# A fixed timetable for the sorted mixtures, three places for gathered rows, and the far bounds of images 0 to 2 moved into the last attention

## The chip, the cores and the metric

The kernel runs on one core of a Trainium2 chip. A core has a matrix engine (PE; its weight loads are listed as PEld), a vector engine (DVE), a scalar engine (ACT), a general engine (POOL), and a queue engine (SP) that issues most of the memory transfers. Each engine takes its own instructions strictly in the order in which they were built; semaphores make one engine wait for another, or for a transfer. The metric is the time of one execution in microseconds (us), the median of several runs. TensorE's clock is granted by a throttle, and the profile reports the granted share (1.0, or 0.5 in stretches where PE has been idle a good deal).

## The reference

Four images of 56 x 56 pixels with 128 channels go through four layers, of which three matter here.

- Layer 2 has a softmax attention over the 3136 pixels of each image, and then a mixture of eight experts: a router picks two experts for each pixel, and the two experts' outputs are added with normalised weights:

```python
top_p, top_i = jax.lax.top_k(router_probs, K)          # K = 2 of 8
expert_out = jnp.einsum('bnd,edc->bnec', x, expert_w) + expert_b
gathered = jnp.take_along_axis(expert_out, top_i[..., None], axis=2)
return jnp.einsum('bnk,bnkc->bnc', top_p, gathered)
```

- Layer 3 starts with an attention whose scores are `exp(-dist2)` of projected queries and keys, followed by a softmax over those scores:

```python
dist2 = q2[:, :, None] + k2[:, None, :] - 2.0 * qk
scores = jnp.exp(-GAMMA * dist2)
attn = jax.nn.softmax(scores, axis=-1)
return jnp.einsum('bqk,bkd->bqd', attn, V)
```

When every query is far from every key all scores are the same number, and the result is the plain mean of the values. The kernel adds that mean, and proves it by bounding all distances (the "bounds"); only if the proof fails does it run the full computation.

- Layer 3 ends with an "expert choice" step: for each of 64 experts the eight pixels with the largest router probability are gathered, sent through the expert, and scattered back.

## The kernel before

**Tiles.** An image is 28 tiles of 112 pixels (`NT`), in seven groups of four (`NG`, 448 columns). The layer-2 attention, `Attention.run` (L2372 on), goes through the four images one after the other. For each group it makes the queries (L2315, `z_ps`), and then takes 25 blocks of 128 keys: a product for the scores (L2339, `s_ps`), an exponential on ACT (L2346), and a product that adds up the results (L2422, `o_ps`). One block is one step; an image has 172 steps. When a group is done, `finish` scales and adds it (L2359 to L2368).

**Work beside the attention.** Everything else of that time is cut into small pieces, which are handed out between the steps. `background(i)` makes the list for the i-th image's attention, and `Paced` hands out the pieces: each piece has a stated cost, the costs are added up along the list, and a piece is due when the attention has done the same share of its first six groups. What is left then is handed out at once. A piece marked as apart waits for the next step if one of the same list has just been handed out. The order in which pieces are handed out is not yet the order of the instructions: a scheduler in the framework places each instruction on its engine by its own estimate of times, and the buffers limit it. One limit matters here: all pieces, the queries of the next group and the `finish` of the last one take their PSUM tile from a single ring of four (`flow.one`, L975), in the order in which they were handed out.

The lists of the four attentions are: for images 0 and 1, an earlier layer's recurrence; for image 2 (the third attention) the sorted mixtures of images 0 and 1, and the far part and the expert choice of image 0; for image 3 (the fourth and last attention) the sorted mixture of image 2, and the far part and the choice of images 1 and 2. Image 3's own mixture and far part follow its attention group by group (`trail`). After the fourth attention come the rest of image 3, the experts, and the scatter.

**The sorted mixture of one image** (`SortedMixture.pieces`) has three parts.

- *front*: statistics, router products and the two best experts of each pixel; then `ranks` and `whose` (L1784 to L1797) compute where each pixel's row goes when rows are sorted by expert. 112 small products (`id_ps`, two instructions each for 56 ids) end in the list of rows, `o_id`.
- *there*: 28 pairs of 128-row tiles. For pair c, `fetch` gathers its rows with two indirect DMAs on POOL (L1805) into a place of the ring "got" and writes them to DRAM (SP, L1809); `load` reads them back block-transposed with four DMAs (SP, L1817) and loads the two experts' weights, whose number is read into a register first (SP, L1825 and L1828); `apply` transposes on DVE (L1834), makes the two products `y_ps` (PE, L1838), copies them (ACT, L1843), and stores them (SP, L1844). That is eight DMAs of SP a pair. In the list, `fetch` of pair c stands with `load` of pair c-5 and `apply` of pair c-8.
- *back*: for each of 28 tiles two indirect DMAs on POOL gather the two experts' rows of each pixel (`bring`, L1852, into a ring of three `o_back` places), and DVE adds them to x (`put`, L1860). It needs all 28 stores of *there*.

The rings lie in one scratch tile: two places for gathered rows ("got"), three for transposed blocks ("xs"), three for weights ("w"), two each for the rest.

**The far part of one image** (`FarAttention.image`): for each group, normalised rows are transposed (L210), projected (L2098, L2103) and given their norms (L2121, L2122); then the mean of the values is added (L2165), and 175 bounds follow (L2134, `d_ps`, 32 x 448), half of them reduced by DVE (L2140) and half by ACT (L2146). **The expert choice of one image** (`ExpertChoice.pieces`) stores x, makes logits (L2600), finds and marks the eight best pixels (L2624 to L2636), gathers them and pools them.

The lists of the two last attentions read:

```python
lists = [
    merged(pieces, front0),
    merged(there0 + back0, front1),
    merged(there1, far0 + merged(add0 + chosen(0), bounds0)),
]                                                        # third
lists = [
    merged(held["back"], front),
    merged(there + back, far1 + merged(add1 + chosen(1), bounds1)),
    far, merged(add + chosen(2), bounds),
]                                                        # fourth
```

Of the kernel before, what the change touches and what calls it, by code (L numbers as in the profile page):

```python
# [40 lines left out]
NQ = EC // ET  # L41
SLOTS = 2 * TOK // 128 + NE - 1

PERIOD = (
# [1598 lines left out]
class SortedMixture:  # L1643

    def __init__(self, env, ctx, flow, mixture, scratch):
# [12 lines left out]
        self.rings, self.turn, at = {}, {}, 0  # L1658
        for name, n in (("got", 2), ("xs", 3), ("xsT", 2), ("w", 3), ("y", 2)):
            self.rings[name] = [scratch[:, at + i * 256 : at + (i + 1) * 256] for i in range(n)]  # L1660
            self.turn[name] = 0
            at += 256 * n
# [25 lines left out]
    def pieces(self, b):  # L1688
# [124 lines left out]
        def load(c):  # L1813
            xs = held["xs", c] = self.ring("xs")
            squares = given.rearrange("(f k) (a i) -> a k f i", k=32, i=32)
            for a in range(4):
                last = nc.sync.dma_start(  # L1817
                    xs[32 * a : 32 * (a + 1), :].rearrange("p (f i) -> p f i", i=32),
                    squares[a][:, 8 * c : 8 * (c + 1), :],
                )  # L1820
            w = held["w", c] = self.ring("w").rearrange("p (j c) -> p j c", j=2)
            for j in range(2):
                at = 2 * c + j
                with env.tc.issue_after(last.ins):
                    e = nc.sync.value_load(  # L1825
                        held["expert"][:, at : at + 1], min_val=0, max_val=NE - 1
                    )
                    last = nc.sync.dma_start(  # L1828
                        w[:, j, :], self.experts[bass.ds(e, 1)].rearrange("e d c -> (e d) c")
                    )  # L1830
# [33 lines left out]

        def lagging(n, *steps):
            listed = []
            last = max(lag for lag, _, _, _ in steps)
            for i in range(n + last):
                for lag, cost, step, apart in steps:
                    if 0 <= i - lag < n:  # L1870
                        listed.append(costing(cost, lambda step=step, i=i - lag: step(i), apart))
            return listed

# [3 lines left out]
        ]  # L1877
        return (
            front,
            lagging(SLOTS // 2, (8, 0.9, apply, True), (5, 0.1, load, False), (0, 2.0, fetch, False)),  # L1880
            lagging(NT, (3, 0.4, put, False), (0, 2.0, bring, False)),
        )

# [25 lines left out]
class Paced:  # L1909
# [6 lines left out]
    def step(self, share):  # L1916

        begun = set()
        while self.at < len(self.pieces):
            piece = self.pieces[self.at]  # L1920
            if share < 1 and (
                self.due[self.at] > self.total * share
                or getattr(piece, "apart", False) and getattr(piece, "list", None) in begun
            ):
                return
            piece()
            begun.add(getattr(piece, "list", None))
            self.at += 1


# [42 lines left out]
class FarAttention:  # L1973
# [16 lines left out]
    def __init__(self, env, ctx, flow, work):  # L1990
# [4 lines left out]

        self.even = ctx.enter_context(ExitStack())
        self.held = [
            stack.enter_context(env.tc.tile_pool(name=name, bufs=1, side="right"))
            for stack, name in ((ctx, "d_odd"), (self.even, "d_even"))
        ]  # L2000
# [66 lines left out]
    def image(self, b, spans, places="d"):  # L2067
# [5 lines left out]
        held = {"q": {}}  # L2073
        pool = self.held[1 - b % 2]

        def turned(g):
            if g == 0:
                held["sums"] = sp.tile([128, NG], F32, tag="x_sums", name="x_sums")
                held["k"] = pool.tile(
                    [128, (NG - 1) * P + LW], BF16, tag="k_near", name="k_near",  # L2080
                    bufs=2 if b % 2 else 1,
                )
# [138 lines left out]
class Attention:  # L2221
# [150 lines left out]
    def run(self, mains, first, background, trail):  # L2372
# [27 lines left out]
        for at in range(-AHEAD, len(steps)):  # L2400
# [12 lines left out]
            if (g, k) == (0, 0):  # L2413
                pieces, following, after = background(i)
                behind = Paced(pieces)
                tails = trail(i)
# [753 lines left out]
def layers_of_safe_scores(env: Env, f, soft):  # L3170
    with ExitStack() as ctx:
# [22 lines left out]
        def background(i):  # L3194
# [11 lines left out]
            elif i == 2:  # L3206
                pieces, out = both([], 3)
                front0, there0, back0 = listed_all(held["sorted"].pieces(0))
                front1, there1, held["back"] = listed_all(held["sorted"].pieces(1))
                far0, add0, bounds0 = mixed(0)  # L3210
                lists = [
                    merged(pieces, front0),
                    merged(there0 + back0, front1),
                    merged(there1, far0 + merged(add0 + chosen(0), bounds0)),
                ]
            else:
                front, there, back = listed_all(held["sorted"].pieces(2))
                far1, add1, bounds1 = mixed(1)
                far, add, bounds = mixed(2)
                lists = [  # L3220
                    merged(held["back"], front),
                    merged(there + back, far1 + merged(add1 + chosen(1), bounds1)),
                    far, merged(add + chosen(2), bounds),
                ]
            return sum(lists, []), out, after

        def mixed(b):
# [6 lines left out]
            )  # L3234

        def listed_all(parts):
            return [listed("mixture", part) for part in parts]

# [40 lines left out]
        with tc.manual_schedule(  # L3279
# [10 lines left out]
            mixing.close()  # L3290
            far.even.close()
            more = ctx.enter_context(tc.tile_pool(name="e_more", bufs=UNITS))
# [118 lines left out]
```

## Time and profile before

| what | us |
|---|---|
| median of 15 runs (2663.25 to 2679.07) | 2669.99 |
| the profiled execution, its own time | 2670.27 |
| its span, first to last instruction | 2668.5 |
| third attention, from its first queries (1216.4) to the fourth's (1767.9) | 551.5 |
| fourth attention, from its first queries to its second group's (1835.1) | 67.2 |
| from there to its last group's queries (2335.7) | 500.6 |
| from there to its last copied result (2422.2) | 86.5 |
| the rest: image 3, the experts, the scatter | 246.3 |

The points in time are those of the PE timeline's `z_ps` rows (L2315), two queries a group, and of DVE's last copy at L2359. An engine's "busy" time counts only executing instructions; a row "A <- B" in a table of waits says that A's engine sat idle until B released it. In the numbers of L2339 and L2422 each product appears as two records, since a 32-bit product takes two passes; a fully busy PE at full clock gets through one such product in 0.75 us (two records each of L2339 and L2422 follow each other every 1.50 us at 1834 to 1839).

### The profile page before, as it was taken

Reading aid. Unit: us, or ns where it says so; the run is one execution under the profiler, and the core shown is the slowest. Engines: PE = TensorE matmul, PEld = TensorE weight load, DVE = VectorE, ACT = ScalarE, POOL = GpSimd, SP = SyncE. Lnnn points to the kernel's source line nnn. Section 1 sums busy time; section 2 is a strip of 40 time slices with the busy share of each in tenths; the row PEclk is TensorE's granted clock in tenths of the full one; section 3 lists DMA queues with packets and bytes.
Section 4 is the critical chain, followed back from the end, with each engine's and each line's share of the span. In section 5 each row is a group of like instructions: output and inputs, shape, how many; then the busy total and the mean of one; then the engine's idle time right before and its main releaser. Section 6 shows DMA issues by size and latency. Waiting matters only on the chain.

```text
span 2668.5 us, 42254 instructions
## 1 busy us (share of the span) xinstructions
PE 2356.4 (88%) x14531; PEld 1296.6 (49%) x14531; DVE 1750.0 (66%) x4986; ACT 1593.1 (60%) x3469; POOL 609.8 (23%) x921
## 2 busy tenths in 40 slices
PE   6999999999999999999855689988989799795586
PEld 4777777764555555555433333444444333232134
DVE  5666999948979597985612547655754475775544
ACT  5999888757666566655322257833355566682584
POOL 4323354200000000000232652343332250011301
PEclk9999999999999999999966788997988699797587
DMA  5000000000000000001144235411143310100575
GB/s 134 14 7 2 2 2 2 2 9 1 1 1 1 1 1 1 1 17 27 50 122 113 58 85 115 97 46 44 50 109 89 72 32 4 25 5 0 170 275 188
DMA packets 248484, 131.74 MB, mean 49 GB/s; under 512 B 119544, under 2 KB 238355, under 8 KB 244164
## 3 DMA queue, kind: packets, MB, share of 16 engines
q1 hardware_dynamic: 236996, 107.23, 15.5%
q0 software_dynamic: 11264, 21.72, 3.1%
q8 instruction: 117, 1.92, 0.3%
q14 instruction: 107, 0.88, 0.1%
HBM read 88.50 MB, written 40.26 MB: 48 GB/s over the span
## 4 chain that ended last, share of the span: by engine, by line
PE 53%; DVE 6%; DMA 6%; ACT 4%; issue 3%; SPq 3%; POOL 3%; POOLq 0%; DVEq 0%; ACTq 0%
PE s_ps L2339 18%; PE o_ps L2422 17%; PE d_ps L2134 3%; DMA o_back<-o_y,o_slot 3%; ACT d_ps L2146 2%; PE xT_ps L210 2%; PE g_ps L1209 2%; PE y_ps L1605 1%; PE y_ps L1838 1%; SPq L1817 1%; PE l_ps L2600 1%; POOL o_back L1852 1%; DMA lot<-in_L_ffn_lots 1%; PE z_ps L2315 1%; PE l_ps L1545 1%
## 5 line engine op out<-in xcount | busy, mean ns | idle before, releaser
L2339 PE MATMUL s_ps<-zT,xnT 128*128 128x448 f32 (+1 forms) x1400 | 668.9, 567 | 14.8 <-DVE zT L2318 14.7
L2346 ACT ACTIVATE e<-s_ps 128x448 f32<-128x448 f32 x688 | 366.6, 542 | 492.1 <-PE s_ps L2339 429.4
L2422 PE MATMUL o_ps<-e,keep 128*128 128x448 f32 (+1 forms) x1376 | 652.0, 558 | 0.0
L2339 PEld LDWEIGHTS s_ps<-zT,xnT 128*128 128x128 f32 (+1 forms) x1400 | 244.4, 193 | 225.9 <-issue 174.8
L2422 PEld LDWEIGHTS o_ps<-e,keep 128*128 128x128 f32 (+1 forms) x1376 | 241.7, 192 | 203.3 <-issue 202.8
L2140 DVE TENSOR_REDUCE found<-d_ps 128x1 f32<-128x448 f32 x306 | 184.5, 618 | 151.8 <-PE d_ps L2134 150.1
L2146 ACT ACTIVATE d_ps<-d_ps,half 128x448 f32<-128x448 f32 (+1 forms) x394 | 238.7, 608 | 74.4 <-PE d_ps L2134 72.6
L1805 POOL DMA_INDIRECT taken<-o_x,o_id x168 | 161.2, 960 | 330.0 <-DMA o_g<-taken 210.4
L2134 PE MATMUL d_ps<-q_near,k_near 32*128 32x448 bf16 (+1 forms) x700 | 165.1, 403 | 43.8 <-ACT d_ps L2146 25.7
L1852 POOL DMA_INDIRECT o_back<-o_y,o_slot x168 | 157.7, 939 | 173.1 <-DMA o_y<-taken 83.8
L210 PE MATMUL xT_ps<-ident,xn 112*128 112x112 f32 x672 | 122.4, 292 | 70.5 <-ACT xn L1966 59.0
L1946 POOL TENSOR_TENSOR g_rs<-var,exponent 112x4 f32<-112x4 f32 x17 | 17.5, 1031 | 647.3 <-DVE var L1945 632.8
L1838 PE MATMUL y_ps<-taken 128*128 128x128 f32 x336 | 82.5, 351 | 81.4 <-DMA taken<-o_w 56.0
L210 PEld LDWEIGHTS xT_ps<-ident,xn 112*128 112x128 f32 x672 | 83.2, 153 | 145.3 <-ACT xn L1966 91.2
L2134 PEld LDWEIGHTS <-k_near 32*128 32x128 bf16 (+1 forms) x700 | 36.4, 94 | 202.7 <-issue 188.7
L1966 ACT ACTIVATE xn<-x,g_off,g_rs 112x128 f32<-112x128 f32 x220 | 92.6, 484 | 65.9 <-DVE g_off L1948 32.8
L1838 PEld LDWEIGHTS y_ps<-taken 128*128 128x128 f32 x336 | 64.8, 233 | 128.1 <-issue 83.1
L1834 DVE STREAM_TRANSPOSE taken<-taken 128x256 f32<-128x256 f32 x84 | 36.5, 438 | 114.8 <-DMA taken<-o_g 109.0
L1843 ACT COPY taken<-y_ps 128x256 f32<-128x256 f32 x84 | 30.9, 368 | 128.5 <-PE y_ps L1838 69.6
L784 PE MATMUL f_ps<-w_fc,h 128*112 128x128 f32 x896 | 104.8, 274 | 1.9 <-ACT h L775 1.6
L679 DVE TENSOR_TENSOR e<-e,band 112x1792 f32<-112x1792 f32 (+3 forms) x56 | 99.9, 1786 | 8.9 <-ACT e L672 8.9
L784 PEld LDWEIGHTS f_ps<-w_fc,h 128*112 128x112 f32 x896 | 99.8, 177 | 5.2 <-ACT h L775 4.8
(481 smaller groups left out, 4501.2 us busy)
## 6 DMA issues: line engine op xcount, KB each, us to landing
lot<-in_L_ffn_lots SPq DMA_DIRECT2D x32, 1024.0 KB
o_g<-taken SPq DMA_DIRECT2D x84, 128.0 KB
taken<-o_g SPq DMA_DIRECT2D x336, 32.0 KB
taken<-o_w SPq DMA_DIRECT2D x168, 64.0 KB
o_y<-taken SPq DMA_DIRECT2D x84, 128.0 KB
out_x<-x SPq DMA_DIRECT2D x28, 224.0 KB
x<-in_x SPq DMA_DIRECT2D x3, 1568.0 KB
o_x<-xn SPq DMA_DIRECT2D x21, 224.0 KB
```

Source lines behind the costliest of these rows:

```text
L210: self.nc.tensor.transpose(ps[:, j * P : (j + 1) * P], xn[:, j, :], self.ident[:P, :P])
L679: nc.vector.tensor_tensor(es, es, bands[stripes[i][1] == 0][:n].rearrange("p h r c -> p h (r c)").unsqueeze(2) .to_broadcast([n, NH, m, 8 ...
L784: nc.tensor.matmul(f_ps[:, j, :], h[:, k, j * P : (j + 1) * P], w_fc2[:, k, :], start=(k == 0), stop=(k == 3),)
L1805: nc.gpsimd.indirect_dma_start(got[:, j, :], None, rows, bass.IndirectOffsetOnAxis(ap=held["id"][:, at : at + 1], axis=0),)
L1838: nc.tensor.matmul(y_ps[:, j, :], xsT[:, j * 128 : (j + 1) * 128], w[:, j, :], start=True, stop=True,)
L1852: nc.gpsimd.indirect_dma_start(back[:, k, :], None, out, bass.IndirectOffsetOnAxis(ap=held["slot"][:, at : at + 1], axis=0),)
L2134: nc.tensor.matmul(d, held["k"][part, 128 * c : 128 * c + n], held["q"][g][part, :], start=True, stop=True,)
L2140: nc.vector.tensor_reduce(self.found[:, self.most : self.most + 1], d, AX.X, ALU.max)
L2146: nc.scalar.activation(d, d, AF.Relu, bias=self.half[:n], accum_out=self.found[:n, self.sums : self.sums + 1],)
L2339: nc.tensor.matmul(s_ps[i * n : (i + 1) * n, :GW], self.xnT[:, at : at + n], zT, start=True, stop=True,)
L2346: nc.scalar.activation(e[:n], s_ps[:n, :GW], AF.Exp)
L2422: nc.tensor.matmul(sums[:, :GW], self.keep[:n, k, :], e[:n], start=(k == 0 and g - 1 not in pairs), stop=last,)
```

## The change

The lists of the third and fourth attention become timetables. `Timed` is a `Paced` whose pieces carry their due times; `placed` gives each step of *there* and *back* a time from a start and a pace, `spread` lays a list evenly between two times, and `timed` sorts them all together. The units are those of a stated total (290 for the third attention, 400 for the fourth), which stands for the first six groups of an attention.

The far part, the choice and the bounds of image 0 leave the third attention; in the fourth they start at 10 of 400, those of image 1 at 112 and those of image 2 at 305. In the third attention the *back* of image 0 (from 178) now overlaps the *there* of image 1 (from 155) instead of preceding it. The loading of the weights becomes a step of its own, six pairs behind `fetch` rather than five, with two places rather than three; "got" has three places rather than two. The k and q tiles of the far part are pooled for images 0 and 3 and for 1 and 2, rather than by odd and even.

```diff
+PLAN = 290, (0, 55), (60, 3.0), (62, 145), (178, 3.4), (155, 4.2)
+LAST = 400, (0, 3.2), (8, 80), (86, 3.4), (212, 2.9), (10, 72), (112, 95), (305, 56)
@@ SortedMixture
-        for name, n in (("got", 2), ("xs", 3), ("xsT", 2), ("w", 3), ("y", 2)):
+        for name, n in (("got", 3), ("xs", 3), ("xsT", 2), ("w", 2), ("y", 2)):
...
             for a in range(4):
-                last = nc.sync.dma_start(
+                held["row"] = nc.sync.dma_start(
...
+        def weights(c):
+            last = held["row"]
             w = held["w", c] = self.ring("w").rearrange("p (j c) -> p j c", j=2)
...
+        def there(start, pace, lead=8):
+            return placed(start, pace, SLOTS // 2, [
+                (lead, lambda c: apply(c), True), (lead - 2, weights, False),
+                (lead - 3, load, False), (0, fetch, False),
+            ], "sorted")
+
+        def back(start, pace):
+            return placed(start, pace, NT, [(3, put, False), (0, bring, False)], "sorted")
...
+def placed(start, pace, n, steps, name):
+    at = []
+    for rank, (lag, step, apart) in enumerate(steps):
+        for i in range(n):
+            piece = costing(0.0, lambda step=step, i=i: step(i), apart)
+            piece.list = name + "_tiles" * apart
+            at.append((start + (i + lag) * pace, rank, piece))
+    at.sort(key=lambda one: one[:2])
+    return [(when, piece) for when, _, piece in at]
+
+def spread(start, end, pieces):
+    due, total = costs(pieces)
+    return [(start + (end - start) * at / total, piece) for at, piece in zip(due, pieces)]
+
+def timed(total, *lists):
+    return Timed(total, sorted(sum(lists, []), key=lambda one: one[0]))
...
+class Timed(Paced):
+    def __init__(self, total, pieces):
+        self.pieces, self.at = [piece for _, piece in pieces], 0
+        self.due, self.total = [when for when, _ in pieces], total
@@ FarAttention.image
-        pool = self.held[1 - b % 2]
+        late = b in (0, B - 1)
+        pool = self.held[0 if late else 1]
@@ background, i == 2
+                lists = timed(
+                    PLAN[0],
+                    spread(0, 0.9 * PLAN[0], pieces),
+                    spread(*PLAN[1], front0), there0(*PLAN[2]),
+                    spread(*PLAN[3], front1), back0(*PLAN[4]), there1(*PLAN[5]),
+                )
+                return lists, out, after
@@ background, else
+                lists = timed(
+                    LAST[0],
+                    held["back"](*LAST[1]), spread(*LAST[2], front2), there2(*LAST[3]),
+                    back2(*LAST[4]),
+                    *[
+                        spread(start, start + 35, far)
+                        + spread(start + 36, start + 75, add + chosen(b))
+                        + spread(start + 36, start + 36 + length, bounds)
+                        for b, (start, length, far, add, bounds) in enumerate((
+                            (*LAST[5], far0, add0, bounds0), (*LAST[6], far1, add1, bounds1),
+                            (*LAST[7], far2, add2, bounds2),
+                        ))
+                    ],
+                )
```

More of the change, by code (lines that the diff above doesn't have):

```diff
@@ L1863, in put @@
                 )
[L1865 to L1872, printed above, removed]
+        def there(start, pace, lead=8):
[5 more added lines that the diff above has]
+            return placed(start, pace, NT, [(3, put, False), (0, bring, False)], "sorted")
         n = 14
@@ L1877, in pieces @@
         ]
[L1878 to L1882, printed above, removed]
+        return listed("mixture", front), there, back
+def placed(start, pace, n, steps, name):
[12 more added lines that the diff above has]
+    return Timed(total, sorted(sum(lists, []), key=lambda one: one[0]))
 def costing(cost, piece, apart=False):
@@ L1994, in __init__ @@
         self.small = ctx.enter_context(env.tc.tile_pool(name="d_small", bufs=2, side="right"))
-        self.even = ctx.enter_context(ExitStack())
+        self.inner = ctx.enter_context(ExitStack())
         self.held = [
             stack.enter_context(env.tc.tile_pool(name=name, bufs=1, side="right"))
-            for stack, name in ((ctx, "d_odd"), (self.even, "d_even"))
+            for stack, name in ((ctx, "d_outer"), (self.inner, "d_inner"))
         ]
@@ L2080, in turned @@
                     [128, (NG - 1) * P + LW], BF16, tag="k_near", name="k_near",
-                    bufs=2 if b % 2 else 1,
+                    bufs=2 if late else 1,
                 )
@@ L2414, in run @@
                 pieces, following, after = background(i)
-                behind = Paced(pieces)
+                behind = pieces if isinstance(pieces, Paced) else Paced(pieces)
                 tails = trail(i)
@@ L3207, in background @@
                 pieces, out = both([], 3)
-                front0, there0, back0 = listed_all(held["sorted"].pieces(0))
-                front1, there1, held["back"] = listed_all(held["sorted"].pieces(1))
-                far0, add0, bounds0 = mixed(0)
[L3211 to L3217, printed above, removed]
-                far1, add1, bounds1 = mixed(1)
[L3219 to L3224, printed above, removed]
+                front0, there0, back0 = held["sorted"].pieces(0)
@@ new lines, in background @@
+                front1, there1, held["back"] = held["sorted"].pieces(1)
+                lists = timed(
[5 more added lines that the diff above has]
+                return lists, out, after
+            else:
+                front2, there2, back2 = held["sorted"].pieces(2)
+                far0, add0, bounds0 = mixed(0)
+                far1, add1, bounds1 = mixed(1)
+                far2, add2, bounds2 = mixed(2)
+                lists = timed(
[12 more added lines that the diff above has]
+                )
+                return lists, None, after
@@ L3234, in mixed @@
             )
-        def listed_all(parts):
-            return [listed("mixture", part) for part in parts]
         def chosen(b):
@@ L3290, in layers_of_safe_scores @@
             mixing.close()
-            far.even.close()
+            far.inner.close()
             more = ctx.enter_context(tc.tile_pool(name="e_more", bufs=UNITS))
```

## The prediction

> **What bounds the kernel now.** I read the page's slices first, then the windows by stage, the waits of PE and POOL, and the timelines of the queues in the third attention.
>
> ```profile
> PE   6999999999999999999855689988989799795586
> PEclk9999999999999999999966788997988699797587
> ```
>
> Each digit is 66.7 us. PE is full until about 1270 us and has holes from there on, which is where the sorted mixtures run; its granted clock falls with it.
>
> ```profile
> core 0: us, PE busy (x) PEld busy (x) DVE busy (x) ACT busy (x) POOL busy (x), PEclk, DMA share, GB/s
> 1216.40:1767.90 551.50, 448.47 (x1675) 227.71 (x1674) 271.58 (x1023) 245.58 (x610) 171.07 (x185) 0.86 0.35 83
> 1767.90:1835.10 67.20, 52.95 (x165) 29.43 (x164) 38.08 (x159) 20.76 (x45) 49.43 (x54) 0.80 0.20 56
> 1835.10:2335.70 500.60, 438.27 (x1539) 190.56 (x1537) 298.63 (x986) 273.76 (x714) 123.95 (x133) 0.86 0.23 52
> 1633.00:1704.70 71.70, 70.66 (x253) 27.86 (x253) 45.04 (x126) 58.64 (x161) 15.84 (x19) 0.91 0.42 90
> ```
>
> The first row is the third attention, the next two are the fourth up to its last group. PE is idle for 103 us of the third and 62 of the third row; ACT has 227 us free there, DVE 202. The last row is one group of the third attention in which PE is never idle: it gives prices of work that fills PE.
>
> ```profile
> PE y_ps L1838 <- DMA taken<-o_w: 50.5, 21, 4.6
> ...
> POOL taken L1805 <- DMA o_g<-taken: 154.3, 42, 29.0
> POOL o_back L1852 <- DMA o_y<-taken: 83.8, 2, 45.9
> ```
>
> PE waits most for the experts' weights. POOL's gathers of pairs wait for the write that frees "got", the gathers of *back* for the last stores (the 83.8 are once in each image).
>
> ```profile
> 1347.91 0.38 SPq L1809 DMA_DIRECT2D o_g<-taken  x1
> 1348.39 0.41 SPq L1844 DMA_DIRECT2D o_y<-taken  x1
> 1348.90 1.94 SPq L1817 DMA_DIRECT2D taken<-o_g  x4
> 1351.65 1.55 SPq L1828 DMA_DIRECT2D taken<-o_w  x2
> 1353.31 0.38 SPq L1809 DMA_DIRECT2D o_g<-taken  x1
> ```
>
> Where pairs follow each other with no attention between, SP is the pace: write to write 1347.91 to 1353.31, 5.4 us a pair, and PE's waits of 3.7 us there are the rest of that period.
>
> ```profile
> 1307.28 1.24 POOL L1805 DMA_INDIRECT taken<-o_x,o_id  x1 [59.96 <-DVE o_id L1797]
> ...
> 1479.82 0.94 POOL L1852 DMA_INDIRECT o_back<-o_y,o_slot  x1 [37.89 <-DMA o_y<-taken]
> 1481.06 0.93 POOL L1852 DMA_INDIRECT o_back<-o_y,o_slot  x1 [0.30 <-issue]
> ...
> 1763.30 0.93 POOL L1852 DMA_INDIRECT o_back<-o_y,o_slot  x1 [45.90 <-DMA o_y<-taken]
> ```
>
> So the third attention is a chain: list of rows (1307), image 0's 28 pairs (to 1480), its 56 back gathers at 1.24 us (to 1550), image 1's 28 pairs (to 1763), and then the fourth attention starts.
>
> **The change, part by part.** The positions below are those of the built order of the changed kernel, engine by engine; the times are from rows of the kernel before.
>
> *Third attention.* (1) Before the first gather stand 73 attention products rather than 67 and three fewer between the ids: +5 us by 0.75 us a product, so 1312. (2) Image 0's pairs took 168.5 us from first write (1311.3) to the first back gather. Four or five writes of image 1 now stand among them on SP, 0.4 us each: +2. *Back* starts near 1487. (3) POOL's order then mixes 56 back gathers of image 0 with 14 of image 1: 70 x 1.24 = 87 us, and 4 for the landing and the write. In this stretch SP stands at the write of pair c+8, which needs the gather behind about 9 back gathers, and behind that write wait the store of pair c, the weights of pair c+2 and, through the store, the next `apply`. So one pair of image 1 takes 11 x 1.24 = 13.6 us there, not 5.4. (4) 13 more writes at 5.45 to 6 us: 75. (5) The last eight results, 5.2 us each: 42. Steps 3 to 5: 208, so image 1's last store is at 1695 rather than about 1761. POOL's and SP's orders hold image 1's back gathers behind that as before. (6) From its first back gather to the fourth attention's second group took 72 us (1763.3 to 1835.1); these gathers now also stand ahead of the second group's queries: 72 to 82. So that group starts at 1695 + 2 + 77 = 1774 instead of 1835: **-61**. Ends: -73 if steps 1 and 2 cost nothing and step 6 stays at 72; -35 if a late weight (1.8 us, below) is paid at each of the seven slow pairs (13), step 6 costs its 82 (5), and one more pair takes 13.6 rather than 5.4 (8).
>
> *The rings and the order on SP.* Weights go from three places and five pairs behind the gather to two places and six. A row of before has a weight load issued at 1346.22 and its product at 1348.37: 2.1 us. Issued two pairs ahead of its use (10.8 us at 5.4) it lands in time: 0. What hides it is that period; if the place comes free only when the previous pair's products end, 1.8 us of landing are bare in some 21 bunched pairs: +38. Nothing excludes a small gain, since 21 waits for weights cost 50.5 us before, but as the wait is the rest of SP's period and SP issues the same eight transfers a pair, I take 0. The third place for gathered rows frees POOL of waits (154.3 us) that it has time for: 0, and if POOL became short there, at most the 1.24 us of a gather a pair, 35. Pooling k and q differently removes no instruction: 0; the wait that it could bring is one far part's last bounds, under 10 us by the next figures.
>
> *Fourth attention.* Image 0's 175 bounds, seven far groups and choice arrive. Their price has two ends.
>
> ```profile
> L2140 DVE TENSOR_REDUCE found<-d_ps 128x1 f32<-128x448 f32 x306 | 184.5, 618 | 151.8 <-PE d_ps L2134 150.1
> L2146 ACT ACTIVATE d_ps<-d_ps,half 128x448 f32<-128x448 f32 (+1 forms) x394 | 238.7, 608 | 74.4 <-PE d_ps L2134 72.6
> ```
>
> Where PE is full: the group of 71.7 us holds 38 attention products (28.5 at 0.75), 20 `y_ps` (7.0 at 0.351), 28 transposes (3.6), 7 logits (5.3), 4 output products and queries (2.2); the other 25.1 are 83 bounds, 0.30 us each. 175 x 0.30 = 52; three far groups whose four transposes, projections and norms count 3 us each on PE, and four nearly free between the first and second group's queries behind the back gathers: 9; the choice 9: **71**. Where ACT must take every second bound, 0.608 + 0.2 for reading its sum, over two bounds: 0.41 each, 72; with seven groups at 4 (28) and a choice whose two searches of 3.4 us are bare (11): 111, and up to 131 if the wait for gathered rows on POOL is bare too. If the bounds lay in PE's idle 62 us they would cost only 9. I take the price of a full PE, because 438 of 500.6 us are full, spread over that share: 71 / 0.876 = **+81**. The built order speaks for it: all 175 bounds stand between the second and fourth group's queries, the 112 id instructions of image 2 and 70 bounds of image 0 follow each other there with no attention product between them, and four instructions of 0.62 us on DVE or 0.81 on ACT cannot hide behind nothing.
>
> *One rule weighed.* PE's clock is halved in this case's rows from 1324.4 to 1379.0 (PEclk 0.50 there), where PE waits 3.7 us a pair. In step 3 PE waits longer, about 8 us a pair, so I expect half clock; the seven attention products between two pairs are 5.3 us at full clock, 10.6 at half, and 10.6 is under 13.6. The sum stands at either clock.
>
> The Trainium skill, page "TensorE: Matmul & The Clock Gate", section "HAM oscillation — how this bites in real kernels", says that gaps on PE above about 3.4 us drop its clock and that this is paid at every gap anew. By that rule the slow stretch would also delay what follows it, some 7 gaps of the page's roughly 1.67 us, 12 us as an estimate; no row here separates this.
>
> *Sum.* The profiled execution took 2670.3 (span 2668.5), the median of the runs is 2670.0, so the execution stands for it. 2670.3 - 61 + 81 = **2690**. Image 3's rest (246.3 us) and the last group (86.5) hold the same work: 0; if fewer bounds of image 2 remain for the last group, some 10 of 86.5 could go, and the same again could come.
>
> **The rivals.**
>
> *A, faster: the fourth attention hides it.* ACT and DVE have 200 us free each and PE 62. If the scheduler's runs are broken up by the engines' waiting, the bounds cost +9 to +20, and the total is 2618 to 2629. It decides from a price below 55 us (61 less the 5 that can be told apart); even PE's bare record, 17.4 us for 84 bounds in the full group, 0.21 each, makes 37 + 18 = 55. Against it stands the run without attention.
>
> *B, faster: back gathers do not hold image 1's pairs.* If POOL issues faster than 1.24 us or SP's writes slip past, image 1's seven pairs go at 5.45, 44 instead of 91 us: -48, 2642. Against: 0.94 busy and 0.30 between in every row, and one strict order on SP.
>
> *C, slower: the weights are late.* Two places only, +38: 2728. For it: 50.5 us of waits for weights before. Against: two periods of slack in SP's order.
>
> *D, no net change.* The third attention gains its 73 and the fourth pays 71 to 75: within 5 us of 2670. That the change does not do what it says is excluded by the built order.
>
> **How the numbers follow.** A change under 0.2% (5.3 us) cannot be told from none. Chances: forecast, with its unknown prices all on the slower side, 0.50; C or a third attention that gains only 35, 0.14; D 0.08; A 0.16; B 0.12. So slower 0.64, same 0.08, faster 0.28. The range goes down to 2635, leaving out most of A, and up to 2742, C with 14 us of bare searches and gathers in the fourth. The forecast's own range is 2676 to 2725.
>
> **What would show it.** Right: the fourth attention's first queries near 1705 and the second group's near 1774; in image 0's *back*, POOL alternating nine back gathers with two of image 1 and PE waiting 7 to 9 us for pairs some five times; some 70 us without an attention product before the fourth's third group; from the second group to the last copy about 668 us rather than 587. Wrong: pairs at 5.4 us through the *back*, attention products between the bounds, or waits for weights longer than 4.6 us.

## The result, and the profile after

The changed kernel takes 2701.18 us (median of 8 runs, 2697.45 to 2707.02), against 2669.97 for the kernel before (median of 40): a ratio of 1.0117, 95% interval 1.0105 to 1.0128, or 31 us. The forecast was 2690. The profiled execution took 2699.5 us (span 2697.6). Its slices:

```profile
PE   6999999999999999999877668789687979996486
PEclk9999999999999999999978778998697969897588
```

The holes of the third attention (slices 20 to 25) are shallower than before; new ones stand in the fourth, from slice 28 on. The windows of the stages, cut at the same queries as before (third attention, fourth up to its second group, from there to its last group):

```profile
core 0: us, PE busy (x) PEld busy (x) DVE busy (x) ACT busy (x) POOL busy (x), PEclk, DMA share, GB/s
1217.60:1705.90 488.30, 387.99 (x1355) 213.26 (x1354) 196.74 (x841) 147.24 (x317) 162.02 (x172) 0.85 0.37 89
1705.90:1783.20 77.30, 57.81 (x230) 31.29 (x228) 45.30 (x203) 33.40 (x83) 50.28 (x54) 0.87 0.19 52
1783.20:2359.10 575.90, 496.35 (x1773) 202.36 (x1771) 363.08 (x1113) 355.70 (x947) 130.36 (x145) 0.84 0.22 49
```

| stage | before | after | difference |
|---|---|---|---|
| third attention | 551.5 | 488.3 | -63.2 |
| fourth, first to second group's queries | 67.2 | 77.3 | +10.1 |
| second to last group's queries | 500.6 | 575.9 | +75.3 |
| last group's queries to the first expert product | 195.9 | 207.3 | +11.4 |
| from there to the end | 136.9 | 131.2 | -5.7 |

With 1.2 us at the start of the third attention these make the 29.1 us between the two spans. The 63 us that the third attention gives up come back as 85 in the fourth (10 and 75) and 11 behind it.

The waits of PE from 1200 to 1830 us:

```profile
PE y_ps L1844 <- DMA taken<-o_w: 49.5, 21, 8.0
PE y_ps L1844 <- DVE taken L1840: 35.0, 6, 8.2
```

The waits for weights add up to what they did before (50.5 us, 21 times). One of them is longer than any before: 8.0 us, at image 0's first pair (1334.25). New are six waits for the transposed rows, five of them of 5.0 to 8.2 us. These six belong to the stretch in which POOL and SP look like this:

```profile
1516.25 0.96 POOL L1808 DMA_INDIRECT taken<-o_x,o_id  x1 [0.30 <-issue]
...
1529.84 0.96 POOL L1808 DMA_INDIRECT taken<-o_x,o_id  x1 [0.30 <-issue]
...
1542.21 0.95 POOL L1808 DMA_INDIRECT taken<-o_x,o_id  x1 [0.30 <-issue]
...
1557.03 0.95 POOL L1808 DMA_INDIRECT taken<-o_x,o_id  x1 [0.31 <-issue]
```

```profile
1527.42 0.38 SPq L1850 DMA_DIRECT2D o_y<-taken  x1
1528.65 1.55 SPq L1834 DMA_DIRECT2D taken<-o_w  x2
1530.30 1.86 SPq L1820 DMA_DIRECT2D taken<-o_g  x4
1534.14 0.38 SPq L1812 DMA_DIRECT2D o_g<-taken  x1
1540.66 0.38 SPq L1850 DMA_DIRECT2D o_y<-taken  x1
```

POOL never pauses there: between two pairs' gathers it issues eight to ten back gathers. SP stands at the write (L1812) until the pair's gathers have landed, and the store and the weights of the pairs ahead stand behind it. A pair takes 12.4 to 14.8 us, as 1516.25 to 1584.32 for five of them shows: 13.6 on average.

In the fourth attention the longest stretch without an attention product lies from 1860.7 to 1941.6, 80.9 us (before, the longest one of the fourth was 56.0). DVE's instructions in it, with their number, busy time, mean, and idle time before them:

```profile
L2175 DVE TENSOR_REDUCE found<-d_ps 128x1 f32<-128x448 f32 x37 | 22.1, 612 | 2.3 <-PE d_ps L2169 2.0
L1791 DVE TENSOR_SCALAR o_high<-o_places,o_highf,o_ids 112x64 f16<-112x64 f16 x55 | 17.4, 318 | 0.0
L1787 DVE TENSOR_SCALAR o_low<-o_places,o_lowf 112x128 f16<-112x128 f16 x54 | 13.4, 248 | 2.9 <-PE id_ps L1795 2.9
```

DVE is busy for 66.5 of these 80.9 us, PE for 55.5 at a clock of 0.58: image 2's ids and image 0's bounds share one engine, and PE waits for both.

### The profile page after: what moved, and what is told of

Read it like the earlier page. It is cut to its first block, busy times and chain, and to the rows that moved or that the text cites. A ratio compares the mean times of both kernels' runs of the same rounds, so it can differ in the third digit from the quotient of the medians.

```text
span 2697.6 us, 42287 instructions
## 1 busy us (share of the span) xinstructions
PE 2363.0 (88%) x14531; PEld 1295.3 (48%) x14531; DVE 1753.2 (65%) x4986; ACT 1597.3 (59%) x3469; POOL 608.4 (23%) x921
## 4 chain that ended last, share of the span: by engine, by line
PE 51%; DVE 6%; DMA 6%; issue 5%; ACT 4%; POOL 4%; SPq 2%; POOLq 0%; DVEq 0%; ACTq 0%
PE s_ps L2374 17%; PE o_ps L2457 17%; DMA o_back<-o_y,o_slot 3%; PE d_ps L2169 3%; PE xT_ps L213 2%; ACT d_ps L2181 2%; PE g_ps L1212 2%; POOL o_back L1858 2%; PE y_ps L1608 2%; PE y_ps L1844 1%; POOL taken L1808 1%; PE l_ps L2635 1%; DMA lot<-in_L_ffn_lots 1%; PE q_ps L2133 1%; PE z_ps L2350 1%
## 5 line engine op out<-in xcount | busy, mean ns | idle before, releaser
L2169 PE MATMUL d_ps<-q_near,k_near 32*128 32x448 bf16 (+1 forms) x700 | 169.6, 407 | 56.7 <-ACT d_ps L2181 24.4
L1844 PE MATMUL y_ps<-taken 128*128 128x128 f32 x336 | 79.9, 343 | 97.1 <-DMA taken<-o_w 49.5
L1866 DVE SCALAR_TENSOR_TENSOR x<-o_back,o_gate,x 112x128 f32<-112x128 f32 x168 | 58.8, 356 | 98.0 <-DMA o_back<-o_y,o_slot 97.8
```

The lines of the kernel that those rows point to most:

```text
L1844: nc.tensor.matmul(y_ps[:, j, :], xsT[:, j * 128 : (j + 1) * 128], w[:, j, :], start=True, stop=True,)
L2169: nc.tensor.matmul(d, held["k"][part, 128 * c : 128 * c + n], held["q"][g][part, :], start=True, stop=True,)
```

## The experiments

These ran on four chips of the same kind, each beside runs of the kernel before on its own chip. On those of runs 0, 2, 5, 6, of runs 1, 3, 4 and of runs 7 to 10 the kernel before takes 2707 to 2711 us, on that of run 11 2674. Which chip the result above comes from is not on record; it is called the first chip here. So ratios are compared; 0.001 is 2.7 us.

| run | ratio to the kernel before, 95% interval | us from it |
|---|---|---|
| 0 the changed kernel again | 1.0216 (1.0196 to 1.0236) | +58 |
| 1 back gathers in turn with the pairs | 1.0098 (1.0067 to 1.0129) | +27 |
| 2 kernel before, the move alone | 1.0211 (1.0185 to 1.0236) | +57 |
| 3 changed kernel without image 0's bounds | 0.9938 (0.9914 to 0.9962) | -17 |
| 4 kernel before without image 0's bounds | 0.9924 (0.9898 to 0.9950) | -21 |
| 5 image 0's bounds spread | 1.0057 (1.0040 to 1.0074) | +15 |
| 6 changed kernel with the old rings | 1.0151 (1.0132 to 1.0171) | +41 |
| 7 runs 1 and 5 together | 0.9929 (0.9906 to 0.9952) | -19 |
| 8 run 7 with the old rings | 0.9899 (0.9877 to 0.9922) | -27 |
| 9 the move alone undone | 1.0132 (1.0108 to 1.0155) | +36 |
| 10 the kernel before again | 0.9994 (0.9977 to 1.0011) | -2 |
| 11 run 8 with image 1's bounds spread | 0.9854 (0.9831 to 0.9878) | -39 |

The last column is the ratio's difference from one times the kernel before on that chip. Where the price of an edit to the changed kernel is given below, it is the difference of two such ratios times 2709, from runs 0 and the edit; where these come from two chips it holds only as far as the two chips agree, and the text says what in the trace supports it.

### Run 0: the changed kernel again

> The changed kernel once more, as the measure for the runs beside it: 1.1 to 1.3% above the kernel before on the same chip.

It came out 1.0216, so on this chip the change costs 58 us where it had cost 31. That was a miss, and it is taken up in the last section; run 0 is the measure for the other edits.

### Run 1: is it the order of gathers on POOL that makes a pair 13.6 us?

```diff
-PLAN = ..., (178, 3.4), (155, 4.2)
+PLAN = ..., (186, 4.2), (155, 4.2)
@@ fetch, of image 1 from pair 8 on
-                nc.gpsimd.indirect_dma_start(got[:, j, :], ...)
+                with env.tc.issue_after(self.gather.ins):     # j == 0
+                    self.gather = nc.gpsimd.indirect_dma_start(got[:, j, :], ...)
@@ bring, of image 0
-                nc.gpsimd.indirect_dma_start(back[:, k, :], ...)
+                with env.tc.issue_after(self.gather.ins):     # k == 0
+                    turn = nc.gpsimd.indirect_dma_start(back[:, k, :], ...)
+            self.gather = turn
```

> The changed kernel with POOL's order of gathers fixed in the stretch of image 0's back: one tile's two back gathers, then one pair's two gathers of image 1, in turn, instead of about nine and two. Theory (the step of 13.6 us a pair): four gathers of 1.24 us are 5.0 us a pair, under SP's 5.4, so the seven slow pairs cost 7 x 5.5 = 39 us rather than the 87 seen from 1497.7 to 1584.3; the fourth attention's first queries come 40 to 48 us earlier than 1705.9, and the total is 2653 to 2665. Rival (SP's own pace or the products hold these pairs anyway): within 8 us of 2701.

Measured: 1.0098, 32 us less than run 0's ratio. POOL's timeline of this run:

```profile
1532.04 0.94 POOL L1809 DMA_INDIRECT taken<-o_x,o_id  x1 [1.20 <-issue]
1533.29 0.95 POOL L1809 DMA_INDIRECT taken<-o_x,o_id  x1 [0.30 <-issue]
1534.55 0.93 POOL L1860 DMA_INDIRECT o_back<-o_y,o_slot  x1 [0.30 <-issue]
1535.78 0.93 POOL L1860 DMA_INDIRECT o_back<-o_y,o_slot  x1 [0.30 <-issue]
1538.40 0.95 POOL L1809 DMA_INDIRECT taken<-o_x,o_id  x1 [1.69 <-issue]
```

This pair takes 6.4 us; from 1526.2 to 1569.5 seven pairs take 6.2 on average. The third attention's sixth group starts 55 us earlier than in run 0 (1565.6 against 1620.3, the query rows of the PE timeline), the fourth attention 32 earlier (1704.0 against 1736.3), and image 1's last store likewise (1697.5 against 1729.8). So the mechanism of the forecast's step 3 is shown (the edit fixes the order, and the pace of *back* in the timetable goes with it), and its price is 32 rather than 40 to 48: the pairs that follow, which run at some 6.7 us a pair in the sixth group instead of 5.5, give 22 back.

### Run 2: the move alone

```diff
 lists = [                                        # third attention
     merged(pieces, front0), merged(there0 + back0, front1),
-    merged(there1, far0 + merged(add0 + chosen(0), bounds0)),
+    there1,
 ]
 lists = [                                        # fourth
     merged(held["back"], front),
-    merged(there + back, far1 + merged(add1 + chosen(1), bounds1)),
+    merged(there + back, far0 + merged(add0 + chosen(0), bounds0)
+                       + far1 + merged(add1 + chosen(1), bounds1)),
```

> The kernel before, in which only the far part, choice and bounds of image 0 go to the fourth attention's list (ahead of image 1's) and k and q are pooled as in the change; no timetable, old rings, old weight loading. Theory (the move costs, the overlap of image 0's back with image 1's pairs pays): image 1's pairs still follow the back, at 5.5 us rather than 7.5 for each, so the third attention gets some 25 to 45 us shorter, the fourth pays 60 to 75: the total is 20 to 45 us above the kernel before. Rival 1 (the timetable brings all the gain of the third): the third stays within 10 us and the total is 55 or more above. Rival 2 (the price lies in the timetable's placing, not in the move): the total is not above the kernel before.

Measured: 1.0211, as much as the whole change costs on that chip (runs 0 and 2 were made together); 57 us is just above the 20 to 45 expected, and at the threshold of the first rival. The stages, against run 10: the third attention takes 537.3 us instead of 574.9 (1218.1 to 1755.4, 1216.3 to 1791.2; the two runs are on two chips), 38 less, so most of the change's gain in the third (55 us in run 0, 519.7 against run 10's 574.9) is to be had without any timetable. From there to the last group's queries it takes 43 us more (634.4 against 591.2), and behind these another 39 (372.0 against 332.6), where 310 bounds now stand instead of 259. (These make 47 us between the two profiled executions; run 10's was the slowest of its ten.) Rival 1 falls with the third attention, rival 2 with the total. The move costs without the timetable too, though in part at other places. The same edit without the new pooling of k and q gives no result: it deadlocks.

### Runs 3, 4 and 5: the price of image 0's bounds, in the fourth, in the third, and spread

```diff
-        assert self.most == self.sums
@@ runs 3 and 4, in background
-                far0, add0, bounds0 = mixed(0)
+                far0, add0, _ = mixed(0)
+                bounds0 = []
@@ run 5 instead
-LAST = 400, (0, 3.2), (8, 80), (86, 3.4), (212, 2.9), (10, 72), (112, 95), (305, 56)
+LAST = 400, (0, 3.2), (8, 80), (86, 3.4), (212, 2.9), (10, 190), (112, 95), (305, 56)
```

> The changed kernel without the 175 bounds of image 0: they are left out, so the proof does not cover image 0. It gives the price of those bounds in the fourth attention. Theory (PE is full: 0.30 us each, spread over a busy share of 0.88): 60 us less, 2641; if ACT is the limit (0.41 each, bare) 72 less, 2629; if they lie in idle time, 10 less or so, 2690.

> The kernel before without the 175 bounds of image 0: they are left out, so the proof does not cover image 0. It gives their price in the third attention. Theory (image 1's 28 pairs took 211 us there against 154 at SP's pace, because bounds lie between them): 35 to 50 us less, 2620 to 2635. Rival (the pairs' transfers hide them): under 10 less.

> The changed kernel with the bounds of image 0 spread over 190 units of the fourth attention's timetable instead of 72, so that 54 rather than 124 of them stand in the second group. Theory (a full PE pays them wherever they are, and the 81 us without an attention product from 1860.7 to 1941.6 are mostly the id instructions on DVE): 5 to 20 us less than the changed kernel. Rival (the bunching is the price): 35 to 60 less, so at or under the kernel before.

Leaving the bounds out saves 0.0278 of the time in the changed kernel, 75 us (the query rows of runs 0 and 3 agree within 6 us up to the fourth's second group, and stand 50 and 74 us apart at the third and fourth), and 0.0076 in the kernel before, 21 us. Per bound that is 0.43 and 0.12 us. The 75 is near the upper end that the forecast had worked out (0.41 each, 72), not the full PE's 0.30 that was taken; the 21 lies between the theory's 35 to 50 and the rival's 10.

Spreading them saves 43 us of the 75, so 32 are left, 0.18 a bound: about what the bare product takes on PE (0.21 in the group of before that PE fills). Here my theory fell and the rival was right: the bunching is more than half of the price. Windows of the second group of the fourth attention, in run 0 and run 5 (same chip):

```profile
1826.40:1984.60 158.20, 130.79 (x462) 50.06 (x460) 111.19 (x377) 95.44 (x252) 27.84 (x33) 0.77 0.17 34
```

```profile
1828.90:1956.40 127.50, 104.56 (x393) 46.77 (x392) 89.82 (x338) 71.87 (x181) 25.87 (x31) 0.80 0.18 36
```

70 bounds fewer stand in that group, and it is 31 us shorter: 0.44 each, with DVE busy for 70% of it in both. The faster chips agree: the changed kernel's second group takes 155.3 us with 124 bounds, that of run 11 124.7 with 54 (70 fewer for 30.6 us, 0.44 each). In the third group another 28 us go (148.1 to 120.6), but only 9 bounds fewer stand there. The rest is something else: in run 0's third group DVE waits for events whose sender the profile does not show ("remote" in its rows).

```profile
DVE gated L1621 <- remote: 11.3, 1, 11.3
DVE found L2175 <- remote: 5.0, 1, 5.0
```

In runs 3 and 5 no such wait of DVE stands there, and on the first chip, where there is none either, the changed kernel takes 131.1 us for the same group. So some 16 of the 75 and of the 43 us may not be the bounds' own; without them the price is 59 us, 0.34 a bound, and about half of it is the bunching. PE's unexplained waits in the second group (14.4 us in run 3, 3.4 in run 0) would put it up again. The 0.44 of the second group is the firmer figure. The later three groups give back 10. The theory's reading of the gap was half right: of 83.9 us in run 0 it shrinks only to 72.4, and in run 3, without these bounds, to 56.7, so most of it is the ids; but the bounds cost far more than the gap shows, in the rest of these two groups as well.

### Run 6: the rings

```diff
-        for name, n in (("got", 3), ("xs", 3), ("xsT", 2), ("w", 2), ("y", 2)):
+        for name, n in (("got", 2), ("xs", 3), ("xsT", 2), ("w", 3), ("y", 2)):
```

> The changed kernel with the rings of before: two places for gathered rows, three for weights. Theory (the rings cost nothing, SP's pace holds the pairs): within 8 us of the changed kernel. Rival (late weights cost 1.8 us in some 21 pairs): 20 to 38 us less.

18 us less than run 0 on the same chip, between the theory's 8 and the rival's 20. The trace says where, though not why: the third group of the fourth attention takes 132.0 us instead of 148.1, and all other stages agree within 6 us. SP's waits there, in run 0:

```profile
SPq L1834 <- PE y_ps L1844: 14.9, 4, 14.0
```

SP stands once for 14 us at a weight load whose place is still held by products that PE has not reached. With three places there is no such row, and on the first chip it was 2.7 us in all, the group taking 131.1. So two places are not paid pair by pair in the bunches, as the rival had it. But SP's stand (2017.5 to 2031.1) begins among the unexplained waits shown above: in this group DVE, ACT and PE wait 16.6, 15.9 and 13.0 us for nothing that the profile shows in run 0, and 1.2, 0.8 and 6.2 in run 6; no wait of PE there over 0.3 us names a weight. So PE is late with these waits, and SP waits for PE. Whether the rings bring these waits on, and what two places cost without them, stays open.

### Runs 7, 8 and 11: the losses taken together

> The changed kernel with both edits together: image 0's back gathers in turn with image 1's pairs, and the bounds of image 0 spread over 190 units. Theory (two separate places of loss, one in the third and one in the fourth attention): the two gains, 37 and 46 us, add up, so this is 15 to 30 us under the kernel before on the same chip, ratio 0.989 to 0.995. Rival (they draw on the same idle time): no better than the better of the two, ratio 1.003 to 1.008.

> The same with the rings of before (two places for gathered rows, three for weights). If the second of two weight places is what costs (19 us in the run with the rings alone), another 10 to 20 us less than with the new rings; if that difference came from places that the other two edits have changed, within 6 us either way.

Run 7 has the edits of runs 1 and 5, run 8 that of run 6 as well. Against run 0's ratio run 7 gains 78 us; 32 and 43 make 75. The two gains add up, as the theory had it, and the kernel is now under the kernel before. The old rings add 8 us on the same chip; the two intervals overlap, so this stays undecided.

```diff
-LAST = ..., (10, 190), (112, 95), (305, 56)
+LAST = ..., (10, 190), (112, 155), (305, 56)
```

> The kernel of the run with turn, spread and old rings (0.990 of the kernel before), with the bounds of image 1 spread over 155 units of the fourth attention's timetable instead of 95. Theory (bounds that follow each other bare cost 0.41 us each on DVE and ACT, spread ones under 0.2): 10 to 25 us less again, ratio 0.981 to 0.986. Rival (image 1's bounds already lie among attention products, or collide with image 0's, which now run until 236 of 400): no gain, 0.988 to 0.994.

Run 11 has this edit on top of run 8: 2635.6 us against 2674.4, ratio 0.9854. It beats both kernels, the first by 1.5% and the second, by the 1.0117 of the first chip, by 2.6%. How much of the step from 0.9899 is image 1's bounds and how much is the chip can't be told: the runs are on two chips, and the change itself differs by 0.010 between chips. The stages on this chip, which took 2674 us for the kernel before, can be set beside those of the first one:

```profile
1222.00:1685.40 463.40, 380.88 (x1355) 210.81 (x1354) 195.25 (x841) 147.07 (x317) 161.38 (x171) 0.87 0.39 94
1685.40:1761.30 75.90, 58.98 (x229) 31.34 (x228) 45.10 (x203) 33.22 (x83) 51.09 (x56) 0.84 0.20 53
1761.30:2296.40 535.10, 477.62 (x1773) 196.31 (x1771) 360.38 (x1113) 352.05 (x947) 130.83 (x145) 0.89 0.25 52
```

The third attention is 25 us shorter than in the changed kernel, and the stretch from the second to the last group 41, with the same number of instructions: PE's share of it rises from 0.86 to 0.89.

### Runs 9 and 10: the move undone, and the kernel before

```diff
-PLAN = 290, (0, 55), (60, 3.0), (62, 145), (178, 3.4), (155, 4.2)
+PLAN = 330, (0, 55), (60, 3.0), (62, 145), (178, 1.6), (160, 4.2)
@@ third attention
+    spread(228, 250, far0), spread(251, 310, add0 + chosen(0)), spread(251, 325, bounds0),
@@ fourth attention
-    (*LAST[5], far0, add0, bounds0), (*LAST[6], far1, add1, bounds1), ...
+    (*LAST[6], far1, add1, bounds1), ...
```

> The changed kernel with the move alone undone: the far part, choice and bounds of image 0 stand in the third attention's timetable (stated total 330, the back of image 0 from 178 at 1.6 a tile, the pairs of image 1 from 160, the far part from 228, choice and bounds from 251 to 325); the fourth keeps its timetable without them. Theory (the move is the loss): the fourth falls back to some 500 us from its second to its last group, the third rises to some 550 to 580, and the total is within 15 us of the kernel before. Rival (the timetable itself loses, wherever the bounds are): 30 us or more above it.

> The kernel before once more, for its stages on the chip of these runs: total within 0.3% of the comparison's own runs; if the experiments' chips differ from the first one in the transfers alone, the attentions of images 0 and 1 (574.6 to 1216.4) take the same time within 1 us and the extra lies from 1300 on.

Run 9 is 36 us above the kernel before, so the theory's 15 is missed and the rival holds for this timetable: from the second to the last group the fourth takes 491.0 us (run 10: 508.5), as expected, but the third takes 634.0 (run 10: 574.9), 59 more rather than none. I had chosen the times of that plan myself, and one plan does not show that every timetable with the far part in the third loses. With run 2, whose third attention is 38 us shorter without any timetable, it speaks for the far part's absence, rather than better times, as what makes the change's third attention short.

Run 10 agrees with its comparison runs. On its chip the first two attentions take the same time as on the first chip within 1 us (574.9 to 1216.3), and the 47 us that the span is longer lie from the third attention's fourth group on.

## Why the prediction was right, step by step

| step | forecast | measured |
|---|---|---|
| 1: first gather | 1312 | 1313.2 |
| 2: first back gather of image 0 | 1487 | 1497.7 |
| 3: 70 mixed gathers on POOL; a pair | 87; 13.6 | 86.6; 13.6 |
| 3: PE's waits for pairs there | 7 to 9, some five | 5.0 to 8.2, five |
| 5: last store of image 1 | 1695 | 1699.4 |
| first queries of the fourth | 1705 | 1705.9 |
| 6: second group's queries | 1774 | 1783.2 |
| fourth, from there to the last copy | 668 | 657.7 |
| run without attention | some 70 | 80.9 |
| behind the last copy | no change | +10.4 |
| total | 2690 | 2699.5 |

**Step 2 was 10 us short.** It took 5 us from step 1 and 2 for SP's extra writes. In the changed kernel the last store of image 0 is issued at 1491.2 instead of 1477.1, 14 later rather than 7: the first store is 4.4 us late, the fourteenth 7.4, the twenty-fourth 9.7, and the last three follow each other every 3.2 to 3.3 us, with writes of image 1 among them, instead of 0.5 and 2.2. What slows the earlier pairs is not shown. The other 4 us are POOL's: the first back gather started 2.7 us after the last store in the kernel before and 6.5 now, since 14 gathers of image 1 stand ahead of the back gathers on POOL, the last four from 1492.7 to 1497.4. That order was counted for SP and not for POOL.

**Step 3, that POOL's 1.24 us a gather holds the pairs, is shown** by the timeline and by run 1, where taking the bunches apart gives 32 us. Rival B (the back gathers do not hold the pairs) falls; its 44 us for seven pairs at 5.45 should have been 38. Steps 4 and 5 made up 6 of the 10 us that step 2 missed.

**Step 6 measured 81.1** from the first back gather of image 1 (1702.1) to the second group's queries; 77 was taken, 82 was the upper end.

**The fourth attention's +81 was the right size for the wrong reason, on the first chip.** Measured are 70.6 to the last copy, and 81.0 to the end (2697.6 less 1783.2, against 2668.5 less 1835.1). But the term was built as 175 x 0.30 plus 18, over PE's share; the runs show 75 us for the bounds alone on the slower chips (59 without the unexplained waits), 0.34 to 0.43 a bound, near ACT's and DVE's price that the forecast kept as the upper end. With the bounds of image 0 left out of both kernels (runs 3 and 4, one chip) the changed one still takes 19 us more from the second to the last group's queries (531.5 against 512.5), about the 18 taken for the far part and the choice, and 13 more behind them. On the slower chips the fourth thus costs some 100 us and not 81 (944.2 against 841.1 from the second group's queries to the end, in runs 0 and 10): that the first chip came to just 81.0 is partly luck. Its argument for a full PE, that 438 of 500.6 us are full, does not hold where the bounds stand: their price goes with how many follow each other, 0.34 to 0.43 in the change's place and 0.18 spread (run 5).

**The term put at nothing, image 3's rest, was 10.4**, probably for the reason that the forecast named as possible: between the last group's queries and the first expert product stand 148 bounds instead of 120. At 0.41 us, 28 more are 11.5, and that stretch is 11.4 longer. Before and after, busy time and idle time of PE's bounds in that stretch account for half of it, 5.7 us of busy time and no idle time; the rest is not shown, and no run takes these 28 away:

```profile
L2134 PE MATMUL d_ps<-q_near,k_near 32*128 32x448 bf16 (+1 forms) x120 | 29.9, 399 | 11.2 <-ACT d_ps L2146 10.0 <-ACT xnT L2086 0.4 <-DVE x L2368 0.2
```

```profile
L2169 PE MATMUL d_ps<-q_near,k_near 32*128 32x448 bf16 (+1 forms) x148 | 35.6, 401 | 11.2 <-ACT d_ps L2181 9.8 <-ACT zT L2630 0.3
```

**Rival A** (the fourth hides the bounds) had its condition right: it decides when the bounds stop following each other. Run 7 is that case, brought about by two edits. **Rival C** (late weights) is not seen on the first chip as it was priced: the waits for weights are 49.5 us in 21 pairs, as before, and not 38 more. But a sign of being wrong that the forecast had named came: a wait for weights longer than 4.6 us, 8.0 at image 0's first pair. It is single, and the first store is 4.4 us late with it. Whether the 18 us of run 6 are late weights stays open.

**The rule weighed, on the clock.** Step 3's stretch was forecast at half clock. The granted clock from 1517.5 to 1584.3 is 0.73: it is 0.50 from 1523.8 to 1537.4, 1.00 from 1537.5 to 1547.6, 0.50 from 1547.7 to 1557.9, and so on. PE's timeline shows the end of the first of these stretches:

```profile
1532.19 0.74 PE L2398 MATMUL y_ps<-s_w_out,oT 128*112 128x129 f32 x2 [3.27 <-DVE inverse L2402]
1532.72 1.70 PE L2374 MATMUL s_ps<-zT,xnT 128*128 128x448 f32 x2
1534.22 1.70 PE L2457 MATMUL o_ps<-e,keep 128*128 128x448 f32 x2
1535.71 1.70 PE L2374 MATMUL s_ps<-zT,xnT 128*128 128x448 f32 x2
1537.20 1.04 PE L2457 MATMUL o_ps<-e,keep 128*128 128x448 f32 x2
1538.08 0.91 PE L2374 MATMUL s_ps<-zT,xnT 128*128 128x448 f32 x2
```

After the wait of 3.27 us, which follows one of 5.04 at 1524.91, a product starts every 1.5 us for some 5 us, and then every 0.75 us again (the clock was half before this wait too); after the wait of 6.47 us that ends at 1551.92 it takes 6. This agrees with the rule of the Trainium skill, page "TensorE: Matmul & The Clock Gate", section "HAM oscillation — how this bites in real kernels", that each long gap is paid anew by a cold start; the page's 1.67 us at half rate is a third of the 5 us seen here, and it counts half of them as lost, so the forecast's estimate of 12 us by it should have been 6. Nothing follows for the sum, since three or four late products, 0.75 us each, are hidden in a pair of 13.6.

## What to carry to other kernels

Work that goes into a stage which looks busy is not priced by that stage's average share, but by what it stands next to: the same bounds cost 0.12 us each among the third attention's pairs, 0.18 spread over the fourth, and 0.34 to 0.43 bunched there. When two gather chains share one queue, look at the order on the queue and not at the sum of its work: bunches of nine gathers held a pair for 13.6 us where turns of two let it pass in some 6. And when work moves from a stage that a chain of transfers bounds, to one that an engine bounds, it can give back little in the first (21 us for the bounds) and cost far more in the second (59 to 75 us), until it is spread (32).

## What the runs showed of the hardware that was not expected

**Chips differ, and not by a factor.** On three of the four chips of the experiments the kernel before takes 37 to 41 us longer than on the first chip, on the fourth of them 4 us longer. On the three the first 1216 us are equal within 4 us, and the change costs 58 us instead of 31 on the one of these where it was run. In the third and fourth attention of these chips' traces PE, ACT and DVE wait at times for nothing that the profile shows. The waits of PE for 1200 to 1830 us in runs 10 (the kernel before) and 0 (the changed one):

```profile
PE s_ps L2339 <- issue: 15.8, 3, 8.0
```

```profile
PE s_ps L2374 <- issue: 24.3, 4, 16.5
```

From 1217 to 2430 us such waits of PE add up to 2.1 us (before) and 8.9 us (changed) on the first chip and 3.3 in run 11, but to 43.8 in run 10 and 65.4 in run 0. The packets of the back gathers are longer too on those chips (mean 221 to 232 ns against 196 for the 3584 bytes of a packet), though in run 11, without the waits, they take 214. The instruction transfers that the trace shows do not end where these waits end, as far as they could be compared in one run (5); what causes them stays open. Each chip was used at one time only, so chip and time cannot be told apart. Where the waits fall differs from run to run of these chips: of the 27 us between 58 and 31, some 16 lie in the fourth attention's third group, which takes 148.1 us in run 0 and 131.1 on the first chip (the kernel before 118.0 in run 10 and 116.7), with the waits of DVE shown under run 5.
